# 22 source tiles and 8 tail buffers in place of 18 and 9, and two pairs of ScalarE instructions put on two schedule steps each

## The chip, the cores and the metric

The kernel runs on one core of one Trainium2 chip. The metric is the device time of one execution in microseconds (us). The instructions of five engines appear in the profile: PE (TensorE, matrix products; PEld is its weight loading), DVE (VectorE), ACT (ScalarE), POOL (GpSimd) and SP (SyncE, which here only issues DMAs and waits for them to be allowed). Each engine works through its own list of instructions in order and waits at semaphores for the others.

## The reference

The input x has shape (2, 256, 128, 128) in float32. Two residual layers follow one another, each on a group-normalised input. The first is the long one: three branches, each a deformable depthwise 3x3 convolution, with dilations 1, 9 and 12. In short:

```python
for w_off, w_def, dil in branches:                 # dil = 1, 9, 12
    off = conv3x3(gn(x), w_off, dil)               # 18 channels: a shift in y and x for each tap
    y = sum over 9 taps of w_def[c, tap] * bilinear(gn(x), position(tap, dil) + off)
    total += gelu(layernorm_c(y))
total += conv1x1(gn(x), conv_w) + conv_b           # 256 -> 256
out = layernorm_c(total)
h = gelu(out @ mlp_w1.T + mlp_b1) @ mlp_w2.T + mlp_b2   # 256 -> 512 -> 256, per pixel
x = x + layernorm_c(h + out)
x = x + conv3x3(gn(x), ternary(weight)) + bias     # second layer
```

## The kernel before

There are three stages. The first (phase A, until about 925 us) normalises x, writes it transposed to DRAM as a table of pixels, computes the offsets and writes the bilinear weights ("hats") to DRAM. The third (phase C, from about 5839 us) is the second layer. The change touches only the second stage, the sampling, in `sample_near`.

**Units.** The sampling walks through units (b, Rt, br): image b, a band of two source rows Rt (66 bands for each image), and branch br; 396 units in all. In each unit:

- `prepare` builds the matrix A of bilinear weights on DVE: for each of up to three rows of taps one product of `hy` and `hx` (L1360). Two A matrices alternate from unit to unit, so the A of unit u+2 can only be written when the matmuls of unit u are through. `hy` and `hx` are loaded by SP (L1340) into three buffers each, one for each of these products.
- `load_tiles` loads the source tiles `xs` of a band (L1319): NT = 11 tiles of 96 pixels by 256 channels, 96 KB each. They are loaded a band ahead and shared by the three branches. All tiles take turns in one set of buffers.
- `sample(u, c)` runs once for each half c of the channels: for every source tile one matmul `pm` = xs x A on PE (L1461) into one of four PSUM banks, an ACT copy of each pair of tiles from the bank to `ev` (L1473, L1481), and then in `accumulate` the weighted additions of the nine taps to the rings of output rows on DVE (L1422, the first one of a row on ACT, L1404). `ev` has three buffers. In the listing, the A of unit u+2 is built after the matmuls of (u, 1) and before the additions of (u, 1).

**Tails.** When four rows of a branch are summed up, a group (b, br, g) begins its tail, a Python generator in `PixelTail.branch`: transposing to pixels (L905, L913, copied by ACT at L921), the statistics of the layer norm (`moments`: L1101 to L1108 on DVE and POOL), normalising and GELU on ACT (`scaled`, L1115); for branch 0 the result is stored to `g12d`, for branch 1 added to it. Branch 2 fetches that sum and goes on: the 1x1 convolution (input `xn` shifted by the negative mean at L1195, product at L1133 and L1137, added at L1145), a second norm, transposing back to channels (`channels`, L1154, copied to `S` at L1214), the first MLP product (L890, L1223), the second (L1137, L1145), a third norm, and the residual addition (L1247, statistics at L1251, store at L1253).

**Schedule steps.** A tail runs piecewise: each `yield` ends a piece, and `yield n, hold, busy` says after how many steps the next piece may come, how many tail buffers the chain holds, and whether the next piece is "busy". `Tail.advance` is one step: it starts a waiting chain where the buffers allow it and runs the next piece of each chain that is due, of the busy ones at most one. It is called twice in each `sample`, at its beginning and in the middle of its tiles, so that a unit has four steps and a group of four rows 24. The pieces are pinned in this order between the instructions of the sampling. Where a ring row is needed again before its tail has read it, `accumulate` calls `advance` until it has.

**Buffers.** `VBUFS` is the number of tail buffers of 4 KB for each partition (tag "v"; v, xn, S, hT and xr come from it), and also the limit in `Tail.may`: the holdings of the running chains plus the next piece's may not exceed it, and for a chain other than the oldest the younger ones' may not exceed `VBUFS - PEAK`. DMAs on SP stand in an order that the framework plans; the compute instructions named above are pinned.

Of the kernel before, what the change touches and what calls it, by code (L numbers as in the profile page):

```python
# [9 lines left out]
F32 = mybir.dt.float32  # L10
# [11 lines left out]
C = 256  # L22
# [20 lines left out]
NT = -(-(W + 2 * REACH) // CI)  # L43
PX = TR * TC
# [5 lines left out]
RINGS = (8, 24, 32)  # L50
BRS = (0, 1, 2)
NORMS = 4
VBUFS = 9
PEAK = 4
GAP = 2
LAG = 7
# [15 lines left out]
def conv_preact_kernel(ctx: ExitStack, tc: tile.TileContext, t: dict, out: bass.AP):  # L72
# [635 lines left out]
    with ExitStack() as actx:  # L708
# [24 lines left out]
        for b in range(NB):  # L733
            stats = ap.tile([P, KC, NGRP, 6], F32, name=f"stats1_{b}", tag=f"stats1_{b}")
            for c in range(KC):
                for g0 in range(0, NGRP, XT):
                    xt = ap.tile([P, XT * NG], F32, name="xt", tag="xt", bufs=3)
# [97 lines left out]
    class Tail:  # L835
# [14 lines left out]
        def may(self, item):  # L850

            others = sum(r[2] for r in self.running if r is not item)
            if self.running and item is not self.running[0]:
                young = others - self.running[0][2] + item[3]
                return young <= VBUFS - PEAK and others + item[3] <= VBUFS
            return others + item[3] <= VBUFS

# [21 lines left out]

        def tile(self, name, tag="v", bufs=VBUFS):  # L880
            return self.pool.tile([P, KC, NG], F32, name=name, tag=tag, bufs=bufs)
# [89 lines left out]
        def branch(self, b, br, g, y):  # L971

            pin = self.pin
            cols = slice(g * NG, (g + 1) * NG)
            gv = g12d[b].rearrange("(k p) f -> p k f", p=P)[:, :, cols]
            z = []
            yield from self.normalised(z, y, (b, br, g))
            v = z[0]
            for c in range(KC):
                pin(  # L980
                    nc.scalar.activation(
                        v[:, c, :], z[1 + c], AF.Gelu,
                        scale=bw[:, br, c : c + 1], bias=bb[:, br, c : c + 1],
                    )
                )
            if br == 0:
                yield 2
                nc.sync.dma_start(gv, v)
                self.stored.add((b, br, g))
                return  # L990
            yield 1, 1 + br
            other = self.tile("other")
            while (b, br - 1, g) not in self.stored:
                yield 1
            nc.sync.dma_start(other, gv)
            if br == 1:
                yield 2
                pin(nc.vector.tensor_tensor(v, v, other, ALU.add))
                yield 2
                nc.sync.dma_start(gv, v)  # L1000
                self.stored.add((b, br, g))
                return
            xn = self.tile("xn")
            nc.sync.dma_start(xn, x[b].rearrange("(k p) h w -> p k (h w)", p=P)[:, :, cols])
            yield 4
            for c in range(KC):
                pin(
                    nc.scalar.activation(
                        xn[:, c, :], xn[:, c, :], AF.Identity, bias=negmean[b][:, c : c + 1]
                    )  # L1010
                )
            yield 1
            yield from self.finish(b, g, v, other, xn)
# [75 lines left out]
    class PixelTail(Tail):  # L1089
# [70 lines left out]
        def branch(self, b, br, g, y):  # L1160

            pin = self.pin
            gv = g12d[b].rearrange("c f -> (c f)").rearrange("(g p e) -> g p e", p=P, e=KC * NG)[g]
            xv = x[b].rearrange("(k p) h w -> p k (h w)", p=P)[:, :, g * NG : (g + 1) * NG]
            yield from self.entered()
            yield 0, 1, True
            v = self.tile("v")
            vf = v.rearrange("p k n -> p (k n)")
            vv = vf.rearrange("p (j c) -> p j c", c=C)
            rows = [vv[:, j, :] for j in range(NG // P)]  # L1170
            self.turned(vv, y, (b, br, g))
            self.read.add((b, br, g))
            rs = self.moments(rows)
            yield 7, 1, True
            yield from self.scaled(rows, rs, AF.Gelu)
            self.norms -= 1
            if br == 0:
                yield 2
                nc.sync.dma_start(gv, vf)
                self.stored.add((b, br, g))  # L1180
                return
            while (b, br - 1, g) not in self.stored:
                yield 1
            if br == 1:
                nc.gpsimd.dma_start(gv, vf, accum_op=ALU.add)
                self.stored.add((b, br, g))
                return
            nc.gpsimd.dma_start(vf, gv, accum_op=ALU.add)
            yield 1, 2
            xn = self.tile("xn")  # L1190
            nc.sync.dma_start(xn, xv)
            yield 4, 2, True
            for c in range(KC):
                pin(
                    nc.scalar.activation(  # L1195
                        xn[:, c, :], xn[:, c, :], AF.Identity, bias=negmean[b][:, c : c + 1]
                    )
                )
            yield 1
            pairs = [(xn[:, c, :], convs[b][:, c, :]) for c in range(KC)]  # L1200
            adds = [self.product("pc1", vv, convb3, pairs, h) for h in range(2)]
            yield 1, 1
            for add in adds:
                add()
            yield 2
            yield from self.entered()
            rs = self.moments(rows)
            yield 7, None, True
            yield from self.scaled(rows, rs, AF.Identity)
            self.norms -= 1  # L1210
            yield 2, 2, True
            S = self.tile("S")
            for c in range(KC):
                pin(nc.scalar.copy(S[:, c, :], self.channels(rows, c)))  # L1214
            yield 1, 3
            hT = []
            for m in range(MC):
                if m % KC == 0:
                    hT.append(self.tile("hT"))
                hp = self.bank("hp")  # L1220
                self.matmul(hp, [(w1[:, c, m * P : (m + 1) * P], S[:, c, :]) for c in range(KC)])
                pin(
                    nc.scalar.activation(  # L1223
                        hT[-1][:, m % KC, :], hp, AF.Gelu, bias=b1[:, m : m + 1]
                    )
                )
                yield 1, 4 if m < MC - 1 else 3
            pairs = [(hT[m // KC][:, m % KC, :], w2[:, m, :]) for m in range(MC)]
            add = self.product("h2", vv, b23, pairs, 0)
            yield 1, 3  # L1230
            add()
            add = self.product("h2", vv, b23, pairs, 1)
            yield 1, 1
            add()
            yield 2, 2
            yield from self.entered()
            rs = self.moments(rows)
            xr = self.tile("xr")
            nc.sync.dma_start(xr, xv)
            yield 7, None, True  # L1240
            yield from self.scaled(rows, rs, AF.Identity)
            self.norms -= 1
            yield 2
            for c in range(KC):
                zc = self.channels(rows, c)
                pin(
                    nc.vector.scalar_tensor_tensor(  # L1247
                        xr[:, c, :], zc, n2w[:, c : c + 1], xr[:, c, :], ALU.mult, ALU.add
                    )
                )  # L1250
                pin(nc.vector.bn_stats(stats2[b][:, c, g, :], xr[:, c, :]))  # L1251
            yield 2, 1
            nc.sync.dma_start(  # L1253
                x1d[b].rearrange("(k p) f -> p k f", p=P)[:, :, g * NG : (g + 1) * NG], xr
            )


    def sample_near(pool, psum, k):
# [50 lines left out]
        def load_tiles(b, Rt):  # L1309

            xts[b, Rt] = []
            for T in range(NT):
                xt = pool.tile([PX, C], F32, name="xs", tag="xs", bufs=18)
                src = bass.AP(
                    table[b].tensor,
                    table[b].offset + (Rt * RI * WT + T * CI) * C,
                    [[C, TC], [WT * C, TR], [1, C]],
                )
                nc.sync.dma_start(xt, src)  # L1319
                xts[b, Rt].append(xt)  # L1320
# [176 lines left out]
        items = [(u, ky) for u in range(len(units)) for ky in taps(u)]  # L1497
        load_hats(0)
        load_tiles(*units[0][0:2])
        load_hats(1)  # L1500
        load_hats(2)
# [113 lines left out]
    with tc.If(beyond > 0) as cmp:  # L1615
        with ExitStack() as bctx:
            psum = bctx.enter_context(tc.tile_pool(name="ps_g", bufs=1, space=PSUM))
            pool = bctx.enter_context(tc.tile_pool(name="gpool", bufs=1))
            for b in range(NB):
                sample_any(b, pool, psum)  # L1620
    with cmp.Else():
        with ExitStack() as bctx:
            psum = bctx.enter_context(tc.tile_pool(name="ps_b", bufs=1, space=PSUM))
            pool = bctx.enter_context(tc.tile_pool(name="bpool", bufs=1))
# [359 lines left out]
```

## Time and profile before

| | |
|---|---|
| three runs | 6616.26, 6634.24, 6640.05 us; median 6634.24 us |
| profiled execution | 6623.9 us, of which its span 6622.0 us |
| instructions | 100200 |
| mean granted TensorE clock | 0.973 |
| PE, DVE, ACT busy | 95%, 87%, 63% of the span |
| first and last matmul of the sampling | at about 925 and 5693 us |

How to read what follows. In a group of instructions, "x17424 | 3238.6, 342 | 168.9 <-" means the number of instructions, their busy time in us, the mean of one in ns, the idle time of the engine just before them in us, and what ended it. In a row of waits, "45.1, 26, 2.2" is the total in us, how often, and the longest. A row of the timeline is start, duration, engine, line, operation, tiles, number of instructions, and in brackets the idle time before it with what ended it. What ended a wait is inferred from semaphore events; where an instruction waits for several, the profile names the one that came last by its own reckoning. A matmul of float32 operands is two instructions in the profile.

### The profile page before, as it was taken

The page shows a single profiled execution, that of the slowest core. Times are in us where ns is not written, and L with a number is a line of the kernel's source. Part 1 is how long each engine was busy: PE and PEld are TensorE (multiplying, and loading weights), DVE is VectorE, ACT ScalarE, POOL GpSimd, SP SyncE. Part 2 cuts the span into 40 slices and gives each one's busy share as a digit, 9 for nine tenths or more (in the row PEclk, how much of TensorE's full clock was granted, in tenths as well). Part 3 has the DMA queues.
Part 4 walks back from the last instruction along what each step waited for, and adds up shares of the span by engine and source line. Part 5 has one row for each costly group of instructions (what it writes and reads, how often), then busy time and mean ns, then how long its engine had stood idle before and what let it go on. Part 6 is the DMA issues. An engine that isn't in the chain of part 4 may idle for free. (4 is left out here: it accounts for less than half of the span.)

```text
span 6622.0 us, 100200 instructions
## 1 busy us (share of the span) xinstructions
PE 6280.3 (95%) x32242; PEld 4993.8 (75%) x32242; DVE 5768.3 (87%) x13644; ACT 4184.2 (63%) x8690; POOL 801.1 (12%) x793
## 2 busy tenths in 40 slices
PE   5999978899999999999998999999999999989999
PEld 3555558888888888888888888888888888734444
DVE  7866667999999999999778999999999999589997
ACT  1344446677777777777676677777777777554442
POOL 0000000111111111111210111111111111200000
PEclk9999978999999999999999999999999999989999
DMA  8976667888878787877677878788877877443332
GB/s 271 284 211 201 205 167 207 212 216 212 219 213 215 211 213 211 221 213 208 177 183 214 217 211 216 211 215 217 219 212 212 218 213 197 108 161 132 138 140 90
DMA packets 626576, 1326.90 MB, mean 200 GB/s; under 512 B 108568, under 2 KB 289320, under 8 KB 609520
## 3 DMA queue, kind: packets, MB, share of 16 engines
q1 hardware_dynamic: 589680, 1218.29, 64.0%
q0 software_dynamic: 18944, 68.46, 5.6%
q10 hardware_dynamic: 17408, 33.56, 1.6%
q8 instruction: 261, 4.28, 0.3%
q14 instruction: 283, 2.32, 0.1%
HBM read 1053.55 MB, written 266.47 MB: 199 GB/s over the span
## 5 line engine op out<-in xcount | busy, mean ns | idle before, releaser
L1461 PE MATMUL pm<-A,xs 96*128 96x216 f32 (+2 forms) x17424 | 3238.6, 342 | 168.9 <-ACT S L1214 45.1
L1461 PEld LDWEIGHTS pm<-A,xs 96*128 96x128 f32 x17424 | 3045.8, 194 | 363.2 <-ACT ev L1473 110.3
L1422 DVE SCALAR_TENSOR_TENSOR ring<-ev,defw,ring 128x256 f32<-128x256 f32 (+4 forms) x6372 | 2478.9, 451 | 90.5 <-ACT ev L1473 52.9
L1473 ACT COPY ev<-pm 128x432 f32<-128x432 f32 (+4 forms) x4488 | 1983.1, 483 | 880.7 <-PE pm L1461 684.0
L1360 DVE TENSOR_TENSOR A<-hy,hx 96x768 f32<-96x768 f32 (+1 forms) x1124 | 1014.8, 946 | 278.5 <-DMA hx<-hats 133.7
L1107 POOL TENSOR_TENSOR rs<-rs,mhalf 128x4 f32<-128x4 f32 x320 | 477.0, 1491 | 3402.8 <-DVE rs L1106 3364.1
L1803 PE MATMUL pc<-cring,signs 128*128 128x512 bf16 x3456 | 759.2, 383 | 17.0 <-ACT cring L1720 7.4
L1115 ACT ACTIVATE v<-v,rs 128x256 f32<-128x256 f32 x1280 | 694.2, 594 | 24.2 <-POOL rs L1108 24.2
L1803 PEld LDWEIGHTS <-signs 128*128 128x128 bf16 x3456 | 340.0, 98 | 435.6 <-issue 29.3
L890 PE MATMUL hp<-S,w 128*128 128x512 f32 x1024 | 500.5, 614 | 1.8 <-ACT S L1214 1.7
L1101 DVE BATCH_NORM_STATS2 st<-v 128x6 f32<-128x256 f32 x1280 | 447.0, 410 | 49.7 <-ACT v L921 49.7
L364 PE MATMUL pz<-wz,xa 128*128 128x486 f32 x1024 | 464.7, 582 | 20.6 <-DVE zr L371 20.4
L1137 PE MATMUL h<-w,hT 128*128 128x256 f32 x2048 | 477.1, 379 | 0.0
L1404 ACT ACTIVATE ring<-ev,defw 128x256 f32<-128x256 f32 (+1 forms) x856 | 404.5, 485 | 24.2
L1137 PEld LDWEIGHTS h<-w,hT 128*128 128x128 f32 x2048 | 369.3, 190 | 65.6 <-issue 1.3
L364 PEld LDWEIGHTS pz<-wz,xa 128*128 128x128 f32 x1024 | 190.8, 193 | 186.2 <-issue 129.0
L921 ACT COPY v<-tp 128x512 f32<-128x512 f32 x384 | 207.7, 597 | 186.3 <-PE tp L913 180.0
L1223 ACT ACTIVATE hT<-hp,b 128x512 f32<-128x512 f32 x256 | 176.0, 688 | 211.4 <-PE hp L890 211.2
L890 PEld LDWEIGHTS hp<-S,w 128*128 128x128 f32 x1024 | 197.3, 198 | 144.2 <-issue 124.6
L470 ACT ACTIVATE hb<-ph 96x512 f32<-96x512 f32 (+1 forms) x384 | 210.1, 596 | 150.8 <-PE ph L463 143.8
L1137 PE MATMUL pc<-convw,xn 128*128 128x256 f32 x1024 | 271.1, 394 | 0.0
L463 PE MATMUL ph<-planes,hatw 128*96 128x512 bf16 (+3 forms) x768 | 219.9, 400 | 20.9 <-DVE planes L453 10.8
(246 smaller groups left out, 4949.0 us busy)
## 6 DMA issues: line engine op xcount, KB each, us to landing
hy<-hats SPq DMA_DIRECT2D x1112, 288.0 KB
hx<-hats SPq DMA_DIRECT2D x1112, 288.0 KB
xs<-tables SPq DMA_DIRECT2D x1452, 96.0 KB
hats<-hb SPq DMA_DIRECT2D x64, 720.0 KB
hats<-hb SPq DMA_DIRECT2D x64, 576.0 KB
xa<-in_x ACTq DMA_DIRECT2D x64, 512.0 KB
xt<-in_x SPq DMA_DIRECT2D x32, 1024.0 KB
tables<-ts SPq DMA_DIRECT2D x64, 512.0 KB
```

What stands on the lines that cost most here:

```text
L364: nc.tensor.matmul(pz[:, 0:NZ], lhsT=xt[:, c, r, :], rhs=k["wz"][:, c, :], start=c == 0, stop=c == KC - 1,)
L890: nc.tensor.matmul(out, lhsT=w, rhs=v, start=i == 0, stop=i == n - 1)
L1101: pin(nc.vector.bn_stats(st[:, j, :], rows[j]))
L1107: nc.gpsimd.tensor_tensor(rs[:, 0, :], rs[:, 0, :], mhalf[:, 0:n], ALU.pow)
L1115: nc.scalar.activation(row, row, func, scale=rs[:, 0, j : j + 1], bias=rs[:, 1, j : j + 1])
L1137: nc.tensor.matmul(bank[:, j, :], lhsT=v[:, px], rhs=w, start=False, stop=i == len(pairs) - 1,)
L1360: nc.vector.tensor_tensor(dst, hy[:, i0:i1].rearrange("p i t w -> p t i w"), hx[:, i0:i1].rearrange("p i t w -> p t i w"), ALU.mult,)
L1404: pin(nc.scalar.mul(dst, src, w))
L1422: pin(nc.vector.scalar_tensor_tensor(dst, src, w, dst, ALU.mult, ALU.add))
L1461: nc.tensor.matmul(pv[:, j, :, m0:m1, :], lhsT=xts[b, Rt][t][:, c * P : (c + 1) * P], rhs=A[:, y0:y1, m0:m1, AO + t * CI : AO + (t + 1) * CI],
L1473: nc.scalar.copy(dst.rearrange("p m (t j) -> p t m j", j=CI), pm[:, 0 : len(ts), 0:n].rearrange("p t (m j) -> p t m j", j=CI),)
L1803: nc.tensor.matmul(pc, lhsT=signs[:, k, (h * 3 + t) * 3 + kx, m * P : (m + 1) * P], rhs=xc[:, i, k, t * JC : (t + 1) * JC, kx : kx + W], s ...
```

## The change

Four edits: `VBUFS` 9 to 8; the buffers of `xs` from 18 to 2 * NT = 22 (a source tile is 1 KB for each partition, so the four more tiles take what the tail buffer gives back); and in the branch 2 tail the two shifts of `xn` and the two transposes and copies to `S` each get a busy step of their own for the second half.

```diff
-VBUFS = 9
+VBUFS = 8
 ...
             yield 4, 2, True
             for c in range(KC):
+                if c:
+                    yield 1, None, True
                 pin(nc.scalar.activation(xn[:, c, :], xn[:, c, :], AF.Identity, ...))
 ...
             yield 2, 2, True
             S = self.tile("S")
             for c in range(KC):
+                if c:
+                    yield 1, None, True
                 pin(nc.scalar.copy(S[:, c, :], self.channels(rows, c)))
 ...
-                xt = pool.tile([PX, C], F32, name="xs", tag="xs", bufs=18)
+                xt = pool.tile([PX, C], F32, name="xs", tag="xs", bufs=2 * NT)
```

Both KC halves are 128 channels. No instruction is added to or taken from the compute engines; a branch 2 tail is two steps longer.

## The prediction

> **What bounds the kernel now.** I read the page first, then the waits of PE and DVE in the steady part of the sampling (1200 to 5630 us), then the timeline around one of the waits, then the windows of the special stretches.
>
> The page: PE is the engine in use nearly all the time, DVE comes next.
>
> ```profile
> PE 6280.3 (95%) x32242; PEld 4993.8 (75%) x32242; DVE 5768.3 (87%) x13644; ACT 4184.2 (63%) x8690; POOL 801.1 (12%) x793
> L1461 PE MATMUL pm<-A,xs 96*128 96x216 f32 (+2 forms) x17424 | 3238.6, 342 | 168.9 <-ACT S L1214 45.1
> ```
>
> The windows: in the steady stretch PE idles 31 of 1700 us (1.8%) with DVE at 93.5%; at the change of image (second row) it idles 24 of 220 us, in the drain of the tails after the last sampling (third) 15 of 130.
>
> ```profile
> 1300.00:3000.00 1700.00, 1668.81 (x8859) 1482.82 (x8858) 1589.76 (x4104) 1244.04 (x2723) 285.37 (x276) 0.99 0.80 215
> 3500.00:3720.00 220.00, 195.77 (x1049) 180.73 (x1048) 200.16 (x495) 151.88 (x347) 23.86 (x23) 0.95 0.79 211
> 5692.00:5822.00 130.00, 114.71 (x499) 77.62 (x498) 56.19 (x201) 64.63 (x122) 26.14 (x39) 0.95 0.33 81
> ```
>
> The waits, 1200 to 5630 us. The largest of PE is put down to the copies of S, which the change splits. Waits for source tiles, which get more buffers, are SyncE's (568.5 us) and not PE's: there PE's weight loads waited 0.3 us for them.
>
> ```profile
> PE pm L1461 <- ACT S L1214: 45.1, 26, 2.2
> PE pm L1461 <- ACT ev L1473: 26.2, 67, 1.2
> PE pm L1461 <- DVE A L1360: 19.2, 10, 4.1
> PE pm L1461 <- ACT ev L1481: 15.4, 27, 2.2
> ...
> DVE A L1360 <- DMA hx<-hats: 100.7, 96, 3.7
> ...
> SPq L1319 <- PE pm L1461: 568.5, 879, 10.2
> ...
> PEld pm L1461 <- DMA xs<-tables: 0.3, 1, 0.3
> ```
>
> The timeline of one of the 26. They return about every 149 us, that is every second group of four rows, nearly all 1.76 us long.
>
> ```profile
> 2082.57 1.82 DVE L1360 TENSOR_TENSOR A<-hy,hx 96x768 f32<-96x768 f32 x2 [0.35 <-PE pm L1461]
> 2085.25 0.95 DVE L1360 TENSOR_TENSOR A<-hy,hx 96x768 f32<-96x768 f32 x1 [0.85 <-DMA hx<-hats]
> 2086.12 3.12 DVE L1422 SCALAR_TENSOR_TENSOR ring<-ev,defw,ring 128x256 f32<-128x256 f32 x8
> 2089.17 1.28 DVE L1145 TENSOR_TENSOR v<-pc,v 128x512 f32<-128x512 f32 x2
> 2090.36 4.00 DVE L1422 SCALAR_TENSOR_TENSOR ring<-ev,defw,ring 128x128 f32<-128x128 f32 x11
> ...
> 2110.96 2.69 DVE L1360 TENSOR_TENSOR A<-hy,hx 96x768 f32<-96x768 f32 x3
> ```
> ```profile
> 2113.00 1.05 ACT L1214 COPY S<-zc 128x512 f32<-128x512 f32 x2
> ...
> 2113.76 3.12 PE L1461 MATMUL pm<-A,xs 96*128 96x216 f32 x10 [1.76 <-ACT S L1214]
> ```
>
> The name in the bracket misleads. This matmul is the first of a unit; in the program's order it waits for the A of that unit and for a bank copied long before, not for S. The third build of A ended at 2110.96 + 2.69 = 2113.65, 0.1 us before the matmul. DVE had worked without a pause since 2085.25. So PE waits here for a DVE that is behind by two units of its work; the S copies only stand nearby. Taking them apart is worth nothing by itself. What counts is where the two extra steps put the DVE work of the tails.
>
> **The change part by part.** All sums are made against the profiled execution, 6623.9 us with a span of 6622.0, which is 10.3 below the median of the three runs, 6634.24. The forecast adds these 10.3 again.
>
> *S in two halves.* Two ACT copies (581 ns each) and eight transposes for each of 64 groups, now 4 + 4 on neighbouring steps: nothing added. The second transposes stand behind half a unit's matmuls, and the MLP product waits one step more; PE has the matmuls of the sampling in between. Bounds: -45 us if the profile's name were right, 0 if it is the build; I take 0, since the build ended last.
>
> *xn in two halves.* 128 shifts of 709 ns on ACT, which is 63% busy. PE's weight loads waited for them 32.6 us in 103 pieces of at most 0.3, PE itself 3.5 us once: between -3.5 and 0; I take 0.
>
> *The schedule.* With two more steps the order of the program changes in the steady part from a pattern of 12 units (two groups) to one of 6. Before, the DVE work of the two groups differed: of the four blocks of norm statistics and the two pairs of additions in the group of the stall, one pair (L1145) and one block lay in the first unit of the slow chain, S spot, residual addition and another block in the second. After, the first unit has the block alone in both groups, the second is as before; the pair of additions has moved a unit ahead, where PE is busy with the MLP and DVE waits for it. PE's work over these units is unchanged. The pair took 2090.36 - 2089.17 = 1.19 us. So this stall shrinks from 1.76 (with the three short waits of 0.13, 0.16 and 0.23 us just before it, 2.28) to 2.28 - 1.19 = 1.1 us.
>
> The other group had no stall before, because its second block of statistics lay a unit later; now it is built alike. Its two units have 16 additions each in place of 19 (bands with 10 of 256 elements in place of 7 of 256 and 6 of 128): 10 x 429 ns against 7 x 429 + 6 x 281 by starts in the timeline, 0.4 us less for each, 0.8 together. Its stall: 1.1 - 0.8 = 0.3. Per pair of groups 2.28 becomes 1.4: 0.9 saved. To it come the waits for `ev` of some 0.4 us in the same groups, with the same cause (ACT waiting for a late DVE); half of it, 0.2. 1.1 x 26 = -29 us. Bounds: all four wait rows gone, -106 us, is too far, since about a third lies outside the steady pattern; the pattern's own is 26 x 2.7 = -70. On the other side a stall of 2.28 + 0.4 in each group, +70. I take -29, from the pair's own duration.
>
> *22 source tiles.* Eleven loads of 96 KB for a band, all now free to start when the band before the last is through; before, four of them had to wait for the current band's last unit. PE waited for none of this, so no direct gain: 0. Indirectly it moves SP's queue. Behind the blocked loads stood those of the hats, and DVE waited 100.7 us for hats; the 0.85 us in the chain above is one of these. Against it, up to ten tiles (0.96 MB) now go out in a row, at 215 GB/s 4.5 us of transfer ahead of the next hats. Both ends: the 0.85 us gone in each of 26 chains, -22; one such wait more in each of 54 groups, +46. Neither is nearer by a row; I take 0 and keep the ends.
>
> *8 tail buffers.* A chain is held back in 20 steps in place of 3, all at the change of image and in the drain; in the steady part the limit never bites. The buffer itself must be free: the tightest is the copy to v (L921), which now waits for a store of x1d (L1253) given 21.4 us of PE work earlier. SP waited at most 7.9 us before such a store, a 512 KB transfer of POOL's took 8.4 to 9.5 us; 17.4 is under 21.4, so 0. In the drain 94 steps in place of 89: the 89 took 129 us, so 5 x 1.45 = +7 at most; with the last two groups now side by side, one norm's wait (4.8 us before the last transposes) may be covered: -5. I take +3, as the youngest chains must wait for buffers. At the change of image, within 24 us idle, +-10; 0.
>
> Sum: 0 + 0 - 29 + 0 + 3 = -26. 6623.9 - 26 = 6598 for an execution like the profiled one, 6608 beside the median.
>
> The Trainium skill (Perfetto Trace Analysis, Identifying Performance Opportunities) reads the same gap returning on the engine that should be full as a possible want of buffers for the next tile. By that rule four more source tiles would take the gap away (-45 us) and one tail buffer less would bring a new one. The row above ends the gap with a DVE build, and tile loads kept PE's weight loads waiting only 0.3 us.
>
> **The rivals.**
>
> - *Full gain.* The stall was just over a threshold, and 1.2 us less, with hats that come earlier, takes DVE out of PE's way in both groups: 26 x 2.7 = -70, +3: 6557, 6567 beside the median. For it: the DVE chain contains a hats wait of 0.85 us. Against: DVE stays above 93% busy.
> - *Nothing.* The work is only shifted, the saving in one group returns in the other: 1.1 + 1.1 + 0.4 is 2.6 against 2.7. 6634 + 3 = 6637. For it: the total DVE work is the same. Against: the lighter bands of the second group.
> - *Slower: hats late in every group.* The burst of tiles puts the third hx load behind it; every chain, now one in each group, waits. Break-even is at 0.55 us for each group over what I assumed (1.1 per pair). At two waits like the one shown, 1.7 us, it is 2 x 1.7 x 26 = +88 - 26 = +62: 6696. For it: DMA queues are 80% used, and SP issues are serial, 0.5 to 0.6 us each. Against: before, tiles also went out up to nine in a row.
>
> **How the numbers follow.** The forecast has 0.42, full gain 0.22, nothing 0.14, slower 0.22. The likeliest alone: 6608, from 6585 to 6628 (its ends -23 and +20 from half of the hats bounds and the drain). The range over all is 6560 to 6690: what lies beyond is part of the first and last rival. A change of 0.5% (33 us) is about what can be told from none: faster is under 6601, slower over 6667. Faster: 0.22 and 0.35 of the forecast's 0.42, 0.37; same: the rest of the forecast and nothing, 0.41; slower 0.22.
>
> **What would show it.** In the changed profile the wait of `pm` put down to S should fall from 45.1 us to 30 or less, its pieces shorter (about 1.1 and 0.3) and now in every group; if the S copies were the cause, it is near 0 while DVE's builds end where they did. SyncE's wait of L1319 for PE should fall well below 568.5 us. DVE's wait for hx tells the rivals apart: 80 to 120 for the forecast, under 60 for the full gain, over 180 for the slower one. The drain should be within 124 to 136 us from the last `pm` to the last store. The prediction fails if PE stalls at places that the old order did not have, or if ACT waits at L921 for a v buffer.

## The result, and the profile after

| | before | after |
|---|---|---|
| median | 6628.32 us (four runs, 6616.26 to 6640.05) | 6729.49 us (four runs, 6720.49 to 6747.89) |
| ratio, 95% interval | 1 | 1.0172 [1.0148, 1.0196] |
| profiled execution's span | 6622.0 us | 6718.6 us |
| sampling, first to last `pm` | 4767.4 us | 4864.4 us |
| before it, between it and the second layer, second layer | 925.3, 146.3, 783.0 us | 918.8, 152.0, 783.5 us |
| within the sampling: sum of PE's idle gaps | 156.9 us | 232.2 us |
| stretches at granted clock 0.5 that begin within the sampling | 177.5 us | 228.7 us |

The kernel became 1.7% slower (the medians above alone give 1.0153, inside the interval), where 0.4% faster was forecast. Nearly all of it lies in the sampling: 97.0 us more. PE idles 75.3 us more there, and at half the clock for 51.2 us more; if half of the latter is lost, an estimate, that is 75.3 + 25.6 = 100.9 us; this comes so near to 97.0 partly by luck (see "What stays open"). The new code shifts the lines by up to four: `pm` is now L1465, the build of A L1364, the hats' loads L1344, the tiles' L1323, the copies to `S` L1218.

The changed kernel's page:

```profile
PE 6306.5 (94%) x32242; PEld 5016.2 (75%) x32242; DVE 5768.9 (86%) x13644; ACT 4182.0 (62%) x8690; POOL 677.5 (10%) x793
L1465 PE MATMUL pm<-A,xs 96*128 96x216 f32 (+2 forms) x17424 | 3264.5, 344 | 243.7 <-issue 117.9
```

Its windows: the steady stretch, and the drain (which is longer by a few us). A row is the window and its length, then the busy time and number of instructions of PE, PEld, DVE, ACT and POOL, the granted clock, the DMA share and GB/s.

```profile
1300.00:3000.00 1700.00, 1625.99 (x8538) 1442.96 (x8538) 1535.03 (x3955) 1198.72 (x2627) 224.84 (x264) 0.98 0.78 207
5782.00:5920.00 138.00, 121.51 (x511) 81.73 (x509) 56.97 (x202) 65.97 (x123) 25.86 (x39) 0.91 0.32 78
```

In the steady stretch PE idles 74 of 1700 us, against 31 before. DVE is less busy than it was (1535 against 1590), though PE waits for it: it does the same work over a longer time.

Its waits, 1200 to 5630 us:

```profile
DVE A L1364 <- PE pm L1465: 171.4, 70, 8.6
PE pm L1465 <- issue: 115.2, 40, 4.0
DVE A L1364 <- DMA hx<-hats: 111.9, 117, 3.0
...
PE pm L1465 <- ACT S L1218: 15.7, 9, 2.0
...
SPq L1323 <- PE pm L1465: 684.9, 908, 7.6
```

The 45.1 us put down to the copies of S have nearly gone, and 115.2 us in 40 pieces stand under "issue", that is, under no named cause. DVE's own waits for PE grew too, from some 120 to 171 us: DVE is now too early in some units of a group and too late in others.

The timeline shows one of the 40. They return about every 77 us: once in nearly every group, where the old stall came in every second.

```profile
2077.39 2.69 DVE L1364 TENSOR_TENSOR A<-hy,hx 96x768 f32<-96x768 f32 x3 [2.09 <-PE pm L1465]
...
2083.34 1.40 DVE L1101 BATCH_NORM_STATS2 st<-v 128x6 f32<-128x256 f32 x4
...
2088.32 1.28 DVE L1145 TENSOR_TENSOR v<-pc,v 128x512 f32<-128x512 f32 x2
2089.52 2.68 DVE L1364 TENSOR_TENSOR A<-hy,hx 96x768 f32<-96x768 f32 x3
...
2101.01 0.95 DVE L1364 TENSOR_TENSOR A<-hy,hx 96x768 f32<-96x768 f32 x1
2102.56 0.95 DVE L1364 TENSOR_TENSOR A<-hy,hx 96x768 f32<-96x768 f32 x1 [0.60 <-DMA hx<-hats]
2104.53 0.95 DVE L1364 TENSOR_TENSOR A<-hy,hx 96x768 f32<-96x768 f32 x1 [1.01 <-DMA hx<-hats]
...
2117.52 2.69 DVE L1364 TENSOR_TENSOR A<-hy,hx 96x768 f32<-96x768 f32 x3
```
```profile
2114.25 0.60 PE L1154 MATMUL zc<-ident,v 128*128 128x128 f32 x4
2114.69 2.24 PE L1465 MATMUL pm<-A,xs 96*128 96x216 f32 x12
2116.76 0.60 PE L1154 MATMUL zc<-ident,v 128*128 128x128 f32 x4
2120.31 3.94 PE L1465 MATMUL pm<-A,xs 96*128 96x216 f32 x10 [2.95 <-issue]
2124.04 2.82 PE L890 MATMUL hp<-S,w 128*128 128x512 f32 x4
```

At 2077.39 DVE had just waited for PE. From there it runs through three units, with 1.61 us of waits for hats and no other wait, and its fourth build ends at 2117.52 + 2.69 = 2120.21; the matmul starts at 2120.31. So the stall is, as before, a wait for A, whatever stands in the bracket. It is the same all along: each of the 51 PE gaps of 1.6 us or more between 1200 and 5600 us ends within 0.15 us after the end of an A build. The chain of late work has become three units long, and the pair of additions (L1145 at 2088.32) and a block of statistics (L1101 at 2083.34) lie inside it. Look also at the PE rows: the first MLP product (L890), PE's own work of the tail, comes only after the stall.

### The profile page after: what moved, and what is told of

It reads as the page before. It is cut to its first block, busy times and chain, and to the rows that moved or that the text cites. A ratio compares the mean times of both kernels' runs of the same rounds, so it can differ in the third digit from the quotient of the medians.

```text
span 6718.6 us, 100327 instructions
## 1 busy us (share of the span) xinstructions
PE 6306.5 (94%) x32242; PEld 5016.2 (75%) x32242; DVE 5768.9 (86%) x13644; ACT 4182.0 (62%) x8690; POOL 677.5 (10%) x793
## 4 chain that ended last, share of the span: by engine, by line
PE 58%; DVE 21%; ACT 8%; DMA 8%; issue 4%; SPq 0%; POOL 0%; DVEq 0%; ACTq 0%; POOLq 0%
PE pm L1465 25%; DVE ring L1426 8%; PE hp L890 7%; PE h L1137 7%; PE pc L1807 6%; PE pz L364 4%; DMA hx<-hats 4%; ACT v L1115 4%; DVE A L1364 3%; ACT ev L1477 3%; DMA xa<-in_x 2%; PE tp L905 2%; PE pc L1137 2%; PE ph L463 2%; DVE st L1101 1%
## 5 line engine op out<-in xcount | busy, mean ns | idle before, releaser
L1465 PE MATMUL pm<-A,xs 96*128 96x216 f32 (+2 forms) x17424 | 3264.5, 344 | 243.7 <-issue 117.9
L1465 PEld LDWEIGHTS pm<-A,xs 96*128 96x128 f32 x17424 | 3051.3, 195 | 433.2 <-ACT ev L1477 156.4
L1364 DVE TENSOR_TENSOR A<-hy,hx 96x768 f32<-96x768 f32 (+1 forms) x1124 | 1017.2, 945 | 331.4 <-PE pm L1465 181.0
L1107 POOL TENSOR_TENSOR rs<-rs,mhalf 128x4 f32<-128x4 f32 x320 | 411.3, 1285 | 3787.6 <-DVE rs L1106 3785.7
L890 PE MATMUL hp<-S,w 128*128 128x512 f32 x1024 | 516.3, 630 | 0.6 <-ACT S L1218 0.5
L1137 PE MATMUL h<-w,hT 128*128 128x256 f32 x2048 | 477.0, 379 | 0.0
L1101 DVE BATCH_NORM_STATS2 st<-v 128x6 f32<-128x256 f32 x1280 | 446.1, 409 | 17.7 <-ACT v L921 17.7
L1137 PEld LDWEIGHTS h<-w,hT 128*128 128x128 f32 x2048 | 369.3, 190 | 66.0 <-issue 1.7
L890 PEld LDWEIGHTS hp<-S,w 128*128 128x128 f32 x1024 | 208.0, 206 | 148.0 <-issue 133.4
L921 ACT COPY v<-tp 128x512 f32<-128x512 f32 x384 | 206.3, 589 | 139.7 <-PE tp L913 136.9
L1137 PE MATMUL pc<-convw,xn 128*128 128x256 f32 x1024 | 257.3, 384 | 1.9 <-ACT xn L1197 1.8
L371 ACT COPY zr<-pz 128x486 f32<-128x486 f32 x128 | 72.3, 565 | 259.4 <-PE pz L364 256.7
```

What stands on the lines that cost most here:

```text
L890: nc.tensor.matmul(out, lhsT=w, rhs=v, start=i == 0, stop=i == n - 1)
L1101: pin(nc.vector.bn_stats(st[:, j, :], rows[j]))
L1107: nc.gpsimd.tensor_tensor(rs[:, 0, :], rs[:, 0, :], mhalf[:, 0:n], ALU.pow)
L1137: nc.tensor.matmul(bank[:, j, :], lhsT=v[:, px], rhs=w, start=False, stop=i == len(pairs) - 1,)
L1364: nc.vector.tensor_tensor(dst, hy[:, i0:i1].rearrange("p i t w -> p t i w"), hx[:, i0:i1].rearrange("p i t w -> p t i w"), ALU.mult,)
L1465: nc.tensor.matmul(pv[:, j, :, m0:m1, :], lhsT=xts[b, Rt][t][:, c * P : (c + 1) * P], rhs=A[:, y0:y1, m0:m1, AO + t * CI : AO + (t + 1) * CI],
```

## The experiments

All times are medians; the ratio is to the kernel before on the same chip, with its 95% interval.

| run | edit against before | time, us | ratio |
|---|---|---|---|
| e1_splits | both splits | 6746.36 | 1.0193 [1.0172, 1.0215] |
| e2_bufs | 22 source tiles, 8 tail buffers | 6578.17 | 0.9942 [0.9922, 0.9961] |
| e3_sonly | S split | 6628.62 | 1.0026 [1.0013, 1.0038] |
| e4_xnonly | xn split | 6526.04 | 0.9877 [0.9849, 0.9904] |
| e5_xn22 | xn split, 22 and 8 | 6512.63 | 0.9834 [0.9806, 0.9862] |
| e6_v8 | 18 and 8 | 6648.35 | 1.0038 [1.0023, 1.0054] |
| e7_cut | all four, less statistics | 6657.71 | 1.0053 [1.0035, 1.0070] |
| e8_xn22lag5 | xn split, 22 and 8, LAG 5 | 6460.56 | 0.9759 [0.9734, 0.9784] |
| e9_after_lag4 | all four, LAG 4 | 6470.18 | 0.9767 [0.9749, 0.9784] |
| e10_after_lag8 | all four, LAG 8 | 6519.16 | 0.9846 [0.9821, 0.9871] |
| e11_before_lag5 | LAG 5 | 6706.52 | 1.0122 [1.0103, 1.0141] |
| e12_bufs_lag5 | 22 and 8, LAG 5 | 6496.64 | 0.9826 [0.9805, 0.9847] |

The kernel before ran at 6612.94 us beside e1 to e4, 6623.29 beside e5 to e8, 6622.63 beside e9 to e11 and 6610.55 beside e12. Of the forecasts printed below, those of e3, e5, e9, e10 and e12 hold the result in their range; e1, e6 and e7 came out just outside; e2, e4 and e8 were faster than forecast, e11 slower.

**Which half of the change costs: e1 and e2.** e1 has the two added `yield` steps and the old buffers, e2 the new buffers and the old steps.

```diff
 # e1_splits: both
             for c in range(KC):
+                if c:
+                    yield 1, None, True
                 pin(nc.scalar.activation(xn[:, c, :], ...
 ...
             for c in range(KC):
+                if c:
+                    yield 1, None, True
                 pin(nc.scalar.copy(S[:, c, :], self.channels(rows, c)))
```

> Only the two splits; buffers as before (18 source tiles, 9 tail buffers). Theory (order of DVE work: with the splits the tails' statistics and additions form one chain of three units in every group, so that A comes late in every group): nearly all of the change, 6705 to 6740 us, PE stalls of 2 to 4 us before a unit's first matmul every 77 us. Rival (buffers: fewer tail buffers and the bursts of source tiles delay the hats): as before, 6615 to 6645 us.

```diff
 # e2_bufs
-VBUFS = 9
+VBUFS = 8
 ...
-  name="xs", tag="xs", bufs=18)
+  name="xs", tag="xs", bufs=2 * NT)
```

> Only the buffers (22 source tiles, 8 tail buffers); S and xn on one step as before. Theory: steady part as before, with one stall of about 1.8 us every second group; 0 to +12 us from the drain and the change of image, 6625 to 6650 us. Rival (buffers): nearly all of the change, 6700 to 6740 us, DVE waiting for hx clearly more than the 100 us of before.

The splits alone cost the whole loss and a little more (1.0193). The buffers alone are a gain of 0.6%, which was not expected. Waits of e1, then of e2, 1200 to 5600 us:

```profile
DVE A L1364 <- DMA hx<-hats: 134.3, 123, 7.1
PE pm L1465 <- issue: 110.9, 38, 4.0
```
```profile
DVE A L1360 <- DMA hx<-hats: 54.3, 61, 2.8
PE pm L1461 <- ACT S L1214: 45.1, 25, 2.2
```

With the old buffers the splits make the same new stalls as in the changed kernel. The new buffers leave the old stalls alone (45.1 us, as before) and halve DVE's waits for hats (54.3 against 100.7). That is a gain, but not at the gap from which the Trainium skill (Perfetto Trace Analysis, Identifying Performance Opportunities) would read a want of buffers: that gap stayed. Of the 52.5 us that e2 saves in the sampling, PE's gaps give 27.1 and half of the half-clock time 22.2 (an estimate): of its 31 gaps of 1.6 us or more, 13 were followed by half the clock, before 24 of 33 (counted as in the last section). Why is not known.

**Which buffers: e6.** It has `VBUFS = 8` alone.

```diff
-VBUFS = 9
+VBUFS = 8
```

> One tail buffer less alone: 18 source tiles, 8 tail buffers, no split. Theory: the steady order is as before's, the drain and the change of image cost some 6 us: ratio 0.999 to 1.003, DVE's waits for hx about 100 us as before; so the gain of the buffers' run is the source tiles'. Rival: the tail limit itself makes the gain: ratio about 0.994.

One tail buffer less costs 0.38%, 25 us by the medians, so the four tiles are worth about 0.9942/1.0038 = 0.990 (e2 over e6, both with 8 tail buffers), or 63 us, in the old order.

**Which split: e3 and e4.** Each has one of the two pairs of added lines, with 18 tiles and 9 tail buffers.

```diff
 # e3_sonly
             for c in range(KC):
+                if c:
+                    yield 1, None, True
                 pin(nc.scalar.copy(S[:, c, :], self.channels(rows, c)))
```

> Only the copies of S on two steps; 18 and 9 buffers, xn on one step. Theory: the order of DVE work differs from both; by sums of DVE and PE work for each unit the chains are a little shorter than before's, so 6590 to 6640 us. Rival (the halved transposes of S themselves make PE or ACT wait): as after, 6700 to 6740 us, and the next run as before.

```diff
 # e4_xnonly
             for c in range(KC):
+                if c:
+                    yield 1, None, True
                 pin(nc.scalar.activation(xn[:, c, :], ...
```

> Only the shifts of xn on two steps; 18 and 9 buffers, S on one step. Theory: by the sums for each unit this order leaves the shortest chains of the four, half the stall of before or less: 6560 to 6615 us. Rival (halved S): 6615 to 6645 us, as before. If the splits cost by being splits, 6650 us and more.

The two do not add up: 1.0026 x 0.9877 is 0.990, both together give 1.0193. The split of S makes the wait that carries its name disappear, and the time does not fall. Waits of e3:

```profile
PE pm L1463 <- issue: 78.5, 28, 3.9
DVE A L1362 <- DMA hx<-hats: 47.5, 56, 4.1
```

So the name was indeed misleading: the same stall stands there under another name, and is longer. The split of xn alone is a gain of 1.2%. The timeline of e4 shows why the second split spoils it. First DVE, then PE, at the place that answers to the one shown above:

```profile
2048.84 2.69 DVE L1362 TENSOR_TENSOR A<-hy,hx 96x768 f32<-96x768 f32 x3
...
2060.35 1.82 DVE L1362 TENSOR_TENSOR A<-hy,hx 96x768 f32<-96x768 f32 x2
2062.89 0.95 DVE L1362 TENSOR_TENSOR A<-hy,hx 96x768 f32<-96x768 f32 x1 [0.72 <-DMA hx<-hats]
...
2075.88 2.69 DVE L1362 TENSOR_TENSOR A<-hy,hx 96x768 f32<-96x768 f32 x3
```
```profile
2071.99 1.04 PE L1154 MATMUL zc<-ident,v 128*128 128x128 f32 x8
2072.87 2.24 PE L1463 MATMUL pm<-A,xs 96*128 96x216 f32 x12
2074.94 1.88 PE L890 MATMUL hp<-S,w 128*128 128x512 f32 x4
2076.66 1.04 PE L905 MATMUL tp<-ident,ring 128*128 128x128 f32 x8
2077.53 0.60 PE L913 MATMUL tp<-extra,S 128*128 128x256 bf16 x4
2078.62 2.09 PE L1463 MATMUL pm<-A,xs 96*128 96x216 f32 x10 [0.49 <-DVE A L1362]
```

DVE does the same work between these builds as in the changed kernel: 27.0 us from the second to the fourth build here, 28.0 there with 0.9 us more of waits for hats. But here all eight transposes to S (`zc`) stand together before the last twelve `pm` instructions shown, and the first MLP product and another group's transposes (2074.94 to 2078.13, 3.2 us) still come before the matmul that needs the late A. They cover DVE's lateness down to 0.49 us. In the changed kernel the second half of S comes one step, a quarter of a unit, later, the MLP product and the transposes behind it move past the waiting matmul, and that cover is gone.

The split of xn also has a gain of its own, which no idle time of PE shows. Here are the waits of the weight loads of the 1x1 product before (1200 to 5630 us), then the first four instructions of that product in one group, before and in the changed kernel:

```profile
PEld pc L1137 <- ACT xn L1195: 32.6, 103, 0.3
```
```profile
2076.23 1.31 PE L1137 MATMUL pc<-convw,xn 128*128 128x256 f32 x4
```
```profile
2081.08 1.03 PE L1137 MATMUL pc<-convw,xn 128*128 128x256 f32 x4
```

Before, weight loads wait in the midst of these four, and they take longer; in e4 2.4 us of these waits are left. From the first of a group's 20 instructions of this product (L1133, L1137) to PE's next instruction it takes, at full clock, a median of 4.22 to 4.30 us in each of the six profiled kernels without the split of xn, and 3.90 us in each of the eight with it: 0.39 us, or 25 us for 64 groups.

**The count of DVE work: e7.** The changed kernel with the statistics at L1255 taken over a quarter of the pixels: two instructions a group of 294 in place of 694 ns, so 0.8 us less of DVE. The second layer's statistics are incomplete there.

```diff
-                pin(nc.vector.bn_stats(stats2[b][:, c, g, :], xr[:, c, :]))
+                pin(nc.vector.bn_stats(stats2[b][:, c, g, :], xr[:, c, 0:W]))
```

> The changed kernel with a shorter DVE chain: the statistics of the last addition (two instructions for each group, 610 ns each) read 128 of 512 columns, so the statistics of the second layer's norm are of a quarter of the pixels. About 0.8 us less DVE work for each group, at the place just before the late A. Theory (PE waits for a DVE that is late with A): stalls shorter by about 0.8 us in each of 54 groups, with the clock 40 to 65 us less than the changed kernel, ratio to before 1.006 to 1.013. Rival (the stall is of the S copies or of PE's own order): under 10 us less, ratio 1.015 to 1.019.

It takes 6657.71 us, 72 less than the changed kernel's median (79 less by the ratios): some 1.1 us for each of 64 groups out of 0.8 us of DVE work. The clock described below may give the rest, which is not shown. If DVE were not what PE waits for, it would be nothing. Waits of e7:

```profile
PE pm L1465 <- ACT S L1218: 45.4, 27, 2.1
PE pm L1465 <- issue: 40.0, 16, 3.1
```

The name "ACT S" is back with nothing changed on ACT, as the stalls became shorter (1.90 us at the group of the timeline, in place of 2.95). The name of this wait tells only which neighbour was last.

**The place alone: e5, e8, e9, e10.** e5 joins e4 and e2, and so is the changed kernel without the split of S: 0.9834 against 1.0172. `LAG` is the number of schedule steps after which a finished group may begin its tail; it moves the tails as a whole against the units, and leaves the work as it is. e8 is e5 with `LAG = 5`, e9 and e10 are the changed kernel with `LAG = 4` and `8`.

```diff
 # e9_after_lag4, on the changed kernel
-LAG = 7
+LAG = 4
```

> xn on two steps, S on one, with 22 source tiles and 8 tail buffers. If the buffers' gain (0.6% alone) comes from hats that arrive earlier and the xn split's (1.2% alone) from shorter DVE chains, they add up only where a hats wait stands in a chain that still holds PE: ratio to before 0.980 to 0.988. If they were the same gain, 0.988; if fewer tail buffers hurt the new order, over 0.99.

> As the run with xn on two steps and 22 and 8 buffers, and a tail begins 5 steps after its rows are complete in place of 7. By the sums for each unit the DVE chains are about the same or a little shorter: ratio to before 0.978 to 0.988, within 0.4% of that run.

> All four edits as in the changed kernel, and LAG 4 in place of 7: every tail begins three steps earlier against the units of the sampling. Theory (only the place of the tails' DVE work against the builds of A counts; counting DVE's work between the builds against PE's work between the units, the three-unit excess of the changed kernel is gone at LAG 4): ratio 0.975 to 0.990, 6460 to 6560 us; no PE wait of 2 to 4 us once in each group. Rival (the splitting of S and the longer tails cost by themselves, wherever they lie): ratio 1.010 to 1.020 as in the changed kernel.

> All four edits, and LAG 8 in place of 7: one step later. Theory (place alone): by the same count of work a small excess is left, so between LAG 4 and the kernel before: ratio 0.980 to 0.998, 6490 to 6610 us. Rival (the splits cost by themselves): 1.010 to 1.020.

The four edits that cost 1.7% at LAG 7 gain 2.3% at LAG 4 and 1.5% at LAG 8. So the four edits do not cost this by themselves; the place that they give the work does. (All of these ratios are to the kernel before at LAG 7; it was not run at 4 or 8.) Waits of e9:

```profile
DVE A L1364 <- DMA hx<-hats: 31.5, 50, 1.2
PE pm L1465 <- DVE A L1364: 0.4, 1, 0.4
```

The 115.2 us under "issue" are gone. In its timeline one unit of DVE's long run without a wait has additions only and no block of statistics. But `LAG` moves the loads too: DVE's waits for hats are 31.5 us here, 27.6 in e8 and 43.7 in e10, so these three do not separate the place of DVE's work from hats that come in time. e5 does so in part: at LAG 7 it has 87.7 us of waits for hats, and PE waits for A only 23.3 us. e8 is the fastest, 2.4% under the kernel before and 4.1% under the changed one; e9 is not to be told from it.

**A miss, and what it showed: e11 and e12.** The same shift on the kernel before, then with the new buffers.

```diff
 # e11_before_lag5
-LAG = 7
+LAG = 5
```

> The kernel before with nothing changed but LAG 5 in place of 7. Theory (place alone): the 26 stalls of 1.76 us go without any split and without other buffers: ratio 0.980 to 0.992, 6490 to 6570 us. Rival (the gain of the best version so far needs the split of xn and 22 source tiles, LAG is worth only its last 0.8%): ratio 0.990 to 1.000.

```diff
 # e12_bufs_lag5
-VBUFS = 9
+VBUFS = 8
 ...
-LAG = 7
+LAG = 5
 ...
-  name="xs", tag="xs", bufs=18)
+  name="xs", tag="xs", bufs=2 * NT)
```

> LAG 5 as in the run before this one, and with it 22 source tiles and 8 tail buffers in place of 18 and 9; no splits. With LAG 5 alone DVE waited 222.7 us for hats, 4.6 us in the chain of every second group, while SP gave out seven tile loads between the hats loads. If the tile loads that wait for a buffer are what holds the hats back, 22 tiles take that away and the gain counted for LAG 5 appears: hx wait under 60 us, ratio 0.975 to 0.990, 6450 to 6560 us. Rival (the order of SP's list puts the tiles before the hats whatever the number of buffers): hx wait stays above 150 us, ratio 1.003 to 1.013.

Against all that was expected, e11 is slower, 1.0122. The count of DVE and PE work between builds, from which it was forecast, holds no transfers. Waits of e11, then its timeline: DVE, and SP's issues before it.

```profile
DVE A L1360 <- DMA hx<-hats: 222.7, 137, 5.0
PE pm L1461 <- DVE A L1360: 102.4, 44, 5.4
```
```profile
2091.51 1.81 DVE L1360 TENSOR_TENSOR A<-hy,hx 96x768 f32<-96x768 f32 x2
2097.96 0.95 DVE L1360 TENSOR_TENSOR A<-hy,hx 96x768 f32<-96x768 f32 x1 [4.63 <-DMA hx<-hats]
```
```profile
2086.86 2.46 SPq L1319 DMA_DIRECT2D xs<-tables  x4
2089.41 0.55 SPq L1340 DMA_DIRECT2D hy<-hats  x1
2090.01 0.59 SPq L1340 DMA_DIRECT2D hx<-hats  x1
2090.69 2.18 SPq L1319 DMA_DIRECT2D xs<-tables  x3
2092.96 0.55 SPq L1340 DMA_DIRECT2D hy<-hats  x1
2093.56 0.59 SPq L1340 DMA_DIRECT2D hx<-hats  x1
2094.24 0.55 SPq L1340 DMA_DIRECT2D hy<-hats  x1
2095.56 0.54 SPq L1340 DMA_DIRECT2D hx<-hats  x1
```

The third `hx` is given out at 2095.56, behind seven tile loads and five hats loads that SP issues nearly without a pause from 2086.86 on; DVE stands 4.63 us for it. Between 2075 and 2112 us SP itself stood 5.6 us at tile loads, in nine waits for PE. With 22 tiles (e12) the waits for hats fall to 29.1 us in 42 pieces, PE's for A to 6.6 us, and the ratio to 0.9826, inside the forecast. So the want of tile buffers does hold the hats back, by blocked tile loads in SP's queue or by the order that is planned around them, which these runs don't tell apart. In this order of the work the four extra tiles are worth 1.0122 - 0.9826 = 3.0% even with one tail buffer less.

## Why the prediction was wrong, point by point

**What bounds the kernel: right.** PE waits for a DVE that is late with A, not for the copies of S: e3 took the name away and not the stall; in e7 less DVE work shortened it and brought the name back; and an A build ends just before each of the long gaps.

**The schedule, -29 us: the step that failed, in sign and size.** The splits alone cost 133 us (6746.36 - 6612.94). Two sentences of this step failed. "The pair of additions has moved a unit ahead, where PE is busy with the MLP and DVE waits for it": the pair and a block of statistics moved into the first unit of a chain that became three units long, and no wait of DVE separates them from it. I had matched DVE's units with PE's by one too few; A is built two units ahead. "PE's work over these units is unchanged": PE's tail work moved too. The split of S moves the first MLP product behind the waiting matmul (2124.04 after a stall that ends at 2120.31), where with the xn split alone it covers DVE (e4). This second one is what costs: e4 has the same long chain and is faster than the kernel before, and e5 shows the changed kernel without the split of S at 0.9834. The forecast of stalls of 1.1 and 0.3 us in turn became a median of 2.7 (2.95 in the one shown) in nearly every group. The bound "a stall of 2.28 + 0.4 in each group, +70" had the right kind of event, and lacked the third unit and the clock.

**S in halves 0, xn in halves 0.** The first can't be told from the schedule that it makes; the second transposes stand behind one step's matmuls (12 instructions of 44), not half a unit's. For xn the range, -3.5 to 0, was too small: the 32.6 us of waits of PE's weight loads were read and not counted, but they made its product longer, and the split takes off 25 us (see e4). The 3.5 us put down to PE are also weight loads' waits. As parts, xn alone is -87 us (e4: 6526.04 - 6612.94) and S alone +16 (e3), and they don't add. The prediction shifted both together and never asked for them apart.

**22 source tiles, 0 (ends -22 and +46).** Mis-sized: about -63 us in the old order (e2 over e6), outside the range taken, while DVE's waits for hats halved, as its better end had it; that the hats give all of it is not shown. The ends counted only the one wait shown in each chain. In the changed order nearly nothing is left of both buffer edits together: 1.0172 over 1.0193, whose intervals overlap. The burst of tiles that was feared to delay the hats did not do so; the lack of buffers did (e11, e12).

**8 tail buffers, +3 (bounds -5 to +7).** Mis-sized: +25 us by the medians of e6; in its trace 7.9 us between sampling and second layer (154.2 against 146.3), just over the upper bound, and 6.4 us in the sampling, taken as 0. No wait of ACT at L921 is put down to a store, as said.

**The signs to look for.** The S wait fell to 15.7 us, under the 30 forecast, for a reason that was not the one given: the stall was longer and got another name. The hats' wait, 111.9 us, lay in the band of the forecast, but this sign misled: little was added to the total, and more of it stood in the chain that makes A late (next paragraph). SyncE's wait for PE at the tiles rose to 684.9 us where a clear fall was forecast; four more tiles alone hardly move it (e2 562.3), and it rises with the splits at 18 tiles too (e1 715.3), for a reason that is not shown. The drain took 135.5 us from the last `pm` to the last store, within 124 to 136.

**The rivals.** The slower one, hats late in every group, holds a part of what happened. It counted 1.7 us of such waits in each chain; the chain shown above has 1.61, and the median over the 51 gaps is 1.9 us (before, 0.95). Its cause is not the one given, the burst of tiles: e1, with 18 tiles, has 2.1 us. These waits are not enough for the loss either: in e5 the chains that end in a gap have 1.6 us of them, and the gaps are short (median 0.6 us). e11 shows the rival's mechanism by itself, at 1.0122. The range ended at 6690, 39 us under the result: the schedule's own bound of +70 was not carried into it, and even that would have given only about 6707.

**What stays open.** Why 22 tiles bring the hats so much earlier in e2 (54.3 us of waits) but not in e5 (87.7) or the changed kernel (111.9), and why e3 has 47.5 with 18, wasn't settled; SP's whole order is planned anew for each kernel. PE's gaps and half the half-clock time account for 131.0 of the 131.7 us that e12 saves in the sampling, 71 of 102 in e4 and 125 of 151 in e9. In the last two the 25 us of the xn split stand beside them, and 6 us or less are left. In the changed kernel these 25 us are saved as well, so that the sum should be about 76, against 97.0 measured: some 20 us are not explained there.

## What to carry to other kernels

Where a schedule interleaves two streams of work on several engines, adding a step moves the work of every engine against every other: redo the sum of each engine's work between two hand-overs, over the whole chain back to the last point where the late engine itself waited, and count the cover that the waiting engine loses as well as the work that the late one gains. Such a sum still lacks the transfers; look up what stands before the needed load in the queue that issues it. When several parts of a change move the same order, try them apart and at other offsets before judging any of them: here the same four edits were worth +1.7% or -2.3% by a single constant. And a wait on the weights' side can make a product longer while the matrix engine counts as busy: compare how long the product takes, not only how long the engine idles.

## What was not expected of the hardware

A short PE gap costs more than itself. In the traces the granted clock is either 1.0 or 0.5, and between 1200 and 5600 us of the kernel before and the changed one the stretches at 0.5 last 3.41 us or twice or four times that. In the kernel before, there, 24 of the 33 gaps of 1.6 us or more had such a stretch begin in them or within 4.5 us after them, and 3 of the 53 between 0.3 and 1.6 us. It is not certain: in the changed kernel it is 33 of 51, in e2 13 of 31. A window of before just after the 1.76 us gap that ends at 2113.76, then one of the changed kernel around the 2.95 us gap that ends at 2120.31 (the clock is the third number from the end):

```profile
2114.60:2118.00 3.40, 3.40 (x9) 2.58 (x8) 3.40 (x10) 1.18 (x3) 0.00 (x0) 0.50 0.94 279
```
```profile
2119.10:2125.90 6.80, 5.59 (x13) 4.36 (x14) 6.80 (x18) 1.28 (x3) 1.48 (x2) 0.50 0.90 223
```

The Trainium skill (TensorE: Matmul & The Clock Gate, HAM oscillation) gives as its rule no PE gaps over some 3.4 us, and reckons the loss as half of the throttled time. By that rule a gap of 1.76 us would cost only itself; the rows above show half the clock after it, so the measurement decides here: a gap well under 3.4 us can bring it. For the loss, half the time is what the trace shows: in the kernel before, `pm` instructions of 96x216 that follow each other start a median of 182 ns apart at clock 1.0 and 360 ns at 0.5.
